# Full-row products on TensorE as two column tiles of 128x64 instead of one of 128x128

## The chip, the cores and the metric

The kernel runs on one core of one Trainium2 chip. The metric is the device time of one execution in microseconds (us). The kernel before takes 568.61 us (median of three runs: 567.25, 568.61 and 568.85).

## What is computed

The program is a cross-attention block in float32. There are 8 batches of 256 query tokens, 256 context tokens and 1024 features in 32 heads of 32. The context serves as keys and as values.

```
x = (hidden - mu) * rsqrt(var + 1e-5) * ln_gamma + ln_beta
Q = split_heads(x @ Wq.T);  K = V = split_heads(ctx)
probs = softmax(where(mask, Q K^T * 32**-0.5, -inf))
out = hidden + (probs @ V) @ Wout.T
```

Everything in it that is a matrix product runs on TensorE: the query product `x @ Wq.T`, the scores `Q K^T`, the values `probs @ V`, and the output product with `Wout`.

## The kernel before

The work is cut into 64 slots, `n` from 0 to 63: 8 batches times 8 groups of 4 heads. The loop `for n in range(N)` writes every engine's work by hand, so that in slot `n` TensorE does, in this order:

- `scores(n + 1)`: 16 products into four PSUM banks, each of 32 rows of the array (one head) by 64 columns (half of a block of 128 queries), with 256 columns of keys streaming through. Its matmuls are on line 487.
- `values(n - 2)`: 32 products of 64 rows by 32 columns, with 128 columns streaming. Line 638.
- products that use all 128 rows and 128 columns of the array, one after another: query products (`first_q`, `make_q` and `query_product`, lines 290, 345 and 447), and output products (`product_steps`, line 722, and `end_steps`, line 789).

From batch 2 on the query product, and from the first batch on the output product, is computed by Strassen's scheme (Winograd's form): 7 half-size products in place of 8, with sums of the operands made by GpSimd (`sum_x`, `sum_at`, `sum_wq`, `sum_wo`). `query_product` makes one of the seven: 16 matmuls of a 128x128 block of weights, with 128 columns of x streaming through each. `product_steps` is called with a list of steps from the table `STEPS`, which spreads 28 matmuls over nine slots. One matmul there has a 128x128 block of attention as its stationary operand and streams 512 columns of Wout.

In float32 each matmul that is written stands in the trace as two MATMUL records and two LDWEIGHTS records (loads of the stationary operand), 8290 of each in all. The stationary operand and the streamed one come from SBUF, the sum lands in PSUM.

The other engines work on the softmax of slot n + 1 (VectorE and ScalarE read the scores out of PSUM, GpSimd divides), copy products out of PSUM, and add the residual. The SyncE queue issues nearly all transfers. Instructions on one engine run in the written order. TensorE's first matmul of a product waits for its operands and for its PSUM bank. The bank tiles that matter: `pq` (one bank, query products, and the first output product of a batch), `po` (one bank, output products), `sc` (four banks, scores), `pv` (two banks, values).

Of the kernel before, what the change touches and what calls it, by code (L numbers as in the profile page):

```python
# [51 lines left out]
P = 128  # L52
# [7 lines left out]
def xattn_kernel(  # L60
# [10 lines left out]
    nc = tc.nc  # L71
# [138 lines left out]
        load_wo(which, pair)  # L210


    xnTs, mvs, rstds = {}, {}, {}

    sts = {}
# [68 lines left out]
    def first_q(s, chunks=range(NC)):  # L284

        if s == 0:
            pqs[0] = ps_q.tile([P, 512], F32, tag="pq", name="pq_0")
        cols = ds(0, P) if s == 0 else ds(P, P + 1)
        for c in chunks:
            nc.tensor.matmul(  # L290
                pqs[0][:, cols], wq[:, 0, c, :], xnT0[:, c, cols],
                start=(c == chunks[0]), stop=(c == chunks[-1]),
            )
        nc.scalar.activation(qa[:, 0, cols], pqs[0][:, cols], AF.Copy, scale=NEG_SCALE)
# [41 lines left out]
    def make_q(n, second=False, chunks=range(NC)):  # L336
        b, o = divmod(n, NQ)
        if chunks[0] == 0:
            if second:
                bank = ps_o.tile([P, 512], F32, tag="po", name=f"pq_{n}")  # L340
            else:
                bank = ps_q.tile([P, 512], F32, tag="pq", name=f"pq_{n}")
            pqs[n] = bank[:, : S + 1] if b == 0 else bank[:, :S]
        for c in chunks:
            nc.tensor.matmul(  # L345
                pqs[n], wq[:, o, c, :], xnTs[b](c), start=(c == 0), stop=(c == NC - 1),
            )

# [34 lines left out]
    def weights(name, o):  # L383

        if name == "ring":
            return ring[:, o]
        first, k = W_AT[name]
        return wq[:, first + o, ds(k, NK)]
# [30 lines left out]
    def x_part(b, name):  # L419

        if name in ("S1", "S3"):
            return sums_x[:, 0]
        if name == "S2":
            return sums_x[:, 1]
        s, k = {"A11": (0, 0), "A12": (0, 1), "A21": (1, 0), "A22": (1, 1), "S4": (1, 0),
                "P1": (0, 0)}[name]
        return to_move[b][:, :, ts(k, NK), s, :].rearrange("p a c k -> p c a k")
# [9 lines left out]
    def query_product(b, p):  # L437
        name, which, begins = Q_PRODUCTS[p]
        if b == SPLIT and name == "A11":
            which = "B11"  # L440
        if begins:
            pqs[b] = ps_q.tile([P, NK, P], F32, tag="pq", name=f"pq_{b}_{name}")
        x_ = x_part(b, name)
        for o in range(NK):
            w = weights(which, o)
            for c in range(NK):
                nc.tensor.matmul(  # L447
                    pqs[b][:, o, :], w[:, c], x_[:, c], start=begins and o + c == 0,
                    stop=c == NK - 1, skip_group_check=True,
                )  # L450
# [232 lines left out]
    def operand(b, name):  # L683

        if name in ("S2", "S1"):
            return s2s[b]
        s, k = {"A11": (0, 0), "A12": (0, 1), "A21": (1, 0), "A22": (1, 1),
                "S3": (1, 0), "S4": (0, 1)}[name]
        return ats[b, k][:, :, s].rearrange("p c a k -> p c (a k)")
# [14 lines left out]
    def product_steps(b, steps):  # L704
        for step in steps:
            p, c = divmod(step, NK)
            name, which, begins = PRODUCTS[p]
            begins = begins or b in P1_ASIDE and name == "A12"
            po = pos.get(b)
            if b == B - 2 and name in ("A12", "S2"):  # L710

                begins = name == "A12"
                if begins and c == 0:
                    po_q[0] = ps_q.tile([P, 512], F32, tag="pq", name=f"po_{b}_{name}")
                po = po_q[0] if begins else po
            elif b in P1_ASIDE and name == "A11":
                if c == 0:
                    p1_pos[b] = ps_q.tile([P, 512], F32, tag="pq", name=f"po_{b}_{name}")
                po = p1_pos[b]
            elif begins and c == 0:  # L720
                po = pos[b] = ps_o.tile([P, 512], F32, tag="po", name=f"po_{b}_{name}")
            nc.tensor.matmul(  # L722
                po, operand(b, name)[:, c], wo[:, which, c],
                start=begins and c == 0, stop=c == NK - 1,
                skip_group_check=not begins,
            )
# [46 lines left out]
    def end_operand(name):  # L773
        return end_sums[name] if name in end_sums else operand(B - 1, name)
# [11 lines left out]
    def end_steps(po, name, which, chunks, begins=(), cols=slice(0, 512)):  # L786

        for c in chunks:
            nc.tensor.matmul(  # L789
                po, end_operand(name)[:, c], wo[:, which, c, cols],  # L790
                start=c in begins, stop=True, skip_group_check=True,
            )
# [100 lines left out]
    nc.gpsimd.tensor_copy(xnT0[:, :, S], bet)  # L893
    ln_norm(0, 1, nc.vector)
    first_q(0, early + late)
    mask_bias(0)
    transpose_x0(1)
# [6 lines left out]
    ])  # L904
    next(first)
    first_q(1)
    make_q(1, second=True, chunks=range(2))
    next(first)
    scores(0, (1,))
    make_q(1, second=True, chunks=range(2, NC))  # L910
    make_q(2)
    for _ in first:
        pass
# [21 lines left out]
    def project_steps(n, place):  # L935
        for one in steps.get((n, place), ()):
            product_steps(*one)


    for n in range(N):  # L940
# [47 lines left out]
        if n in products:  # L988
            query_product(*products[n])
            copies.append(partial(copy_product, *products[n]))  # L990
# [67 lines left out]
        if N - NQ + 2 < n < N - 1:  # L1058

            c = n - (N - NQ + 3)  # L1060
            if c == 0:
                last = ps_q.tile([P, 512], F32, tag="pq", name="po_last")
            end_steps(last, "A11", B11, (c,), (0,))
# [20 lines left out]
    for c in range(2):  # L1084
        end_steps(to_c11, "A12", B21, (c,), (0,))
        end_steps(to_c21, "A22", T4, (c,), (0,))
# [78 lines left out]
```

## Time and profile before

The profiled execution took 567.12 us; its span from the first to the last instruction is 565.3 us.

| engine | busy us | share of the span | instructions |
|---|---|---|---|
| TensorE matmuls (PE) | 560.3 | 99% | 8290 |
| TensorE weight loads (PEld) | 385.3 | 68% | 8290 |
| VectorE (DVE) | 467.0 | 83% | 1716 |
| ScalarE (ACT) | 423.8 | 75% | 1464 |
| GpSimd (POOL) | 395.7 | 70% | 636 |

The granted TensorE clock is full (0.999). The 16 DMA engines moved 211 GB/s on average. Matmuls are pipelined: a record lasts longer than the distance to the next one, so the pace of a stream is read from starts, or from how long a run of equal matmuls takes, and not from the mean length of one.

### The profile page before, as it was taken

How to read it: one execution, taken by the hardware profiler on the slowest of the kernel's cores; microseconds unless marked ns; L12 is line 12 of the kernel's file. 1: busy time of each engine (PE TensorE's matmuls, PEld its weight loads, DVE VectorE, ACT ScalarE, POOL GpSimd, SP SyncE). 2: the span in 40 equal slices, each digit the busy share in tenths (PEclk: the TensorE clock that was granted, in tenths of full speed). 3: DMA queues.
4: the chain of work that ended last, by engine and by line, in shares of the span. 5: the costliest groups of instructions: out<-in, count | busy, mean ns of one | idle time of the engine just before them, and what ended most of it. 6: DMA issues, size and time to landing. Idle time of an engine off the chain costs nothing.

```text
span 565.3 us, 22379 instructions
## 1 busy us (share of the span) xinstructions
PE 560.3 (99%) x8290; PEld 385.3 (68%) x8290; DVE 467.0 (83%) x1716; ACT 423.8 (75%) x1464; POOL 395.7 (70%) x636
## 2 busy tenths in 40 slices
PE   8999999999999999999999999999999999999997
PEld 8777775767766767667766776667766767754454
DVE  5889889999897988978888888988888877879923
ACT  3699989997767866787777867778776876769920
POOL 2688887899777666867568665777648657448780
PEclk9999999999999999999999999999999999999999
DMA  8967667966698677877779667887658874536651
GB/s 310 397 178 203 173 188 216 296 179 177 199 311 255 206 196 228 253 206 207 206 225 283 191 174 221 242 264 197 172 155 257 244 202 134 149 105 183 205 169 74
DMA packets 47228, 119.17 MB, mean 211 GB/s; under 512 B 8976, under 2 KB 9744, under 8 KB 47120
## 3 DMA queue, kind: packets, MB, share of 16 engines
q1 hardware_dynamic: 46976, 117.74, 69.9%
q8 instruction: 66, 1.08, 0.9%
q14 instruction: 42, 0.34, 0.2%
q10 hardware_dynamic: 144, 0.01, 0.0%
HBM read 66.33 MB, written 11.53 MB: 138 GB/s over the span
## 4 chain that ended last, share of the span: by engine, by line
PE 82%; POOL 5%; DVE 5%; ACT 3%; issue 2%; DMA 2%; SPq 0%; DVEq 0%; POOLq 0%; ACTq 0%
PE po_S L722 21%; PE pq_A L447 19%; PE pv L638 11%; PE sc L487 10%; PE po_A L722 10%; PE pq_S L447 8%; PE po_end L789 3%; ACT e L530 2%; POOL e L545 2%; DVE e L526 2%; DVE pT L551 2%; PE po_last L789 1%; DMA pT<-pT 1%; POOL wo L182 1%; POOL wq L366 1%
## 5 line engine op out<-in xcount | busy, mean ns | idle before, releaser
L545 POOL TENSOR_SCALAR e<-e,rden 128x256 f32<-128x256 f32 x466 | 216.6, 483 | 123.2 <-DVE rden L537 120.6
L530 ACT ACTIVATE e<-e,mn 128x256 f32<-128x256 f32 x512 | 254.1, 502 | 45.2 <-DVE mn L526 44.8
L551 DVE STREAM_TRANSPOSE pT<-e 128x512 f32<-128x512 f32 x256 | 178.9, 704 | 36.6 <-POOL e L545 32.3
L526 DVE CUSTOM_DVE_ANT_0 e<-sc,mb 128x256 f32<-128x256 f32 x512 | 185.2, 415 | 24.8 <-PE sc L487 24.5
L557 ACT COPY pc<-pT 128x512 f32<-128x512 f32 x128 | 79.0, 617 | 55.3 <-DVE pT L551 35.7
L530 ACT ACTIVATION_READ_ACCUMULATOR e<-e,mn 128x1 f32 x512 | 98.5, 192 | 0.0
L638 PEld LDWEIGHTS pv<-pT,v 64*32 64x32 f32 x4096 | 57.1, 105 | 25.7 <-ACT pc L557 11.5
L722 PE MATMUL po_S<-wo,at 128*128 128x512 f32 x152 | 74.3, 606 | 0.0
L638 PE MATMUL pv<-pT,v 64*32 64x128 f32 x4096 | 74.2, 274 | 0.0
L487 PE MATMUL sc<-k,qa 32*64 32x256 f32 x2048 | 71.9, 387 | 0.1
L487 PEld LDWEIGHTS sc<-k,qa 32*64 32x64 f32 x2048 | 37.7, 131 | 45.5 <-issue 32.1
L722 PE MATMUL po_A<-wo,at 128*128 128x512 f32 x128 | 59.4, 605 | 0.0
L345 PE MATMUL pq<-xnT,wq 128*128 128x256 f32 (+1 forms) x240 | 55.0, 384 | 0.1
L447 PEld LDWEIGHTS pq_A<-xnT,wq 128*128 128x128 f32 x416 | 48.5, 192 | 6.2 <-issue 5.0
L345 PEld LDWEIGHTS pq<-xnT,wq 128*128 128x128 f32 x240 | 44.6, 190 | 8.5 <-issue 1.2
L722 PE MATMUL po_S<-wo,s 128*128 128x512 f32 x104 | 50.2, 607 | 0.0
L447 PE MATMUL pq_A<-xnT,wq 128*128 128x128 f32 x416 | 48.5, 275 | 0.0
L537 DVE RECIPROCAL rden<-den 128x2 f32<-128x2 f32 x256 | 38.1, 149 | 6.6 <-ACT e L530 5.6
L526 DVE DVE_READ_ACCUMULATOR2_ANT mn<- 128x1 f32 x512 | 42.4, 83 | 0.0
L722 PEld LDWEIGHTS po_A<-wo,at 128*128 128x128 f32 x128 | 22.9, 189 | 25.7 <-issue 24.7
L722 PEld LDWEIGHTS po_S<-wo,at 128*128 128x128 f32 x152 | 25.5, 190 | 19.6 <-issue 19.6
L755 POOL TENSOR_TENSOR r<-r,p 128x512 f32<-128x512 f32 x24 | 30.7, 1281 | 4.8 <-DMA r<-in_x_dram 3.9
(102 smaller groups left out, 666.7 us busy)
## 6 DMA issues: line engine op xcount, KB each, us to landing
v<-in_kv_dram SPq DMA_DIRECT2D x32, 512.0 KB, 4.6
pT<-pT SPq DMA_DIRECT2D x128, 128.0 KB, 3.2
pT<-pc SPq DMA_DIRECT2D x128, 128.0 KB, 4.3
ring<-kept_T SPq DMA_DIRECT2D x20, 512.0 KB, 5.5
k<-in_kv_dram SPq DMA_DIRECT2D x32, 256.0 KB, 4.2
x<-in_x_dram SPq DMA_DIRECT2D x15, 512.0 KB, 5.6
r<-in_x_dram SPq DMA_DIRECT2D x28, 256.0 KB, 5.0
out_dram<-r SPq DMA_DIRECT2D x28, 256.0 KB, 3.5
```

The source lines that it names most:

```text
L345: nc.tensor.matmul(pqs[n], wq[:, o, c, :], xnTs[b](c), start=(c == 0), stop=(c == NC - 1),)
L447: nc.tensor.matmul(pqs[b][:, o, :], w[:, c], x_[:, c], start=begins and o + c == 0, stop=c == NK - 1, skip_group_check=True,)
L487: nc.tensor.matmul(scs[n][j][ts(w, P // 2), s, :], qa[r, n % NQ, ds(s * P + w * P // 2, P // 2)], ks[n - n % 2][r, n % 2, :], start=True, ...
L526: nc.vector.tensor_tensor_reduce(out=e[:, s, :], in0=pss[j][:, s, :], in1=mbs[n // NQ], scale=1.0, scalar=NO_SCORE, op0=ALU.add, op1=ALU.m ...
L530: nc.scalar.activation(e[:, s, :], e[:, s, :], AF.Exp, bias=mn[:, s : s + 1], scale=-1.0, accum_out=den[:, s : s + 1],)
L537: nc.vector.reciprocal(rden, dens[j])
L545: engine.tensor_scalar(es[j][:, s, :], es[j][:, s, :], rden[:, s : s + 1], 1.0, ALU.mult, ALU.mult,)
L551: nc.vector.transpose(pT[:, :, :, j, :, :].rearrange("p a i s k -> p (a i) s k"), es[j].rearrange("p s (b t) -> p b s t", t=K),)
L557: nc.scalar.copy(pc[:, :, ts(j, 2)], pT[:, 1, :, ts(j, 2)])
L638: nc.tensor.matmul(pvs[n][r][j * HD : (j + 1) * HD], vs[n - n % 2][ts(r, 2 * K), i, ds(n % 2 * P + j * HD, HD)], pT[ts(r, 2 * K), :, i, j, ...
L722: nc.tensor.matmul(po, operand(b, name)[:, c], wo[:, which, c], start=begins and c == 0, stop=c == NK - 1, skip_group_check=not begins,)
L755: nc.gpsimd.tensor_tensor(r, r, p1s[b], ALU.add)
```

## The change

A helper `product(out, stationary, moving)` takes the place of `nc.tensor.matmul` at the five places that use the whole array. It writes two matmuls. The first has columns 0 to 63 of the stationary block and writes PSUM partitions 0 to 63; the second has columns 64 to 127 and writes partitions 64 to 127. Both stream the same moving operand, and both carry the same start and stop flags.

```diff
+    def product(out, stationary, moving, **flags):
+
+        for w in range(2):
+            nc.tensor.matmul(
+                out[ts(w, P // 2)], stationary[:, ts(w, P // 2)], moving, **flags
+            )
+
@@ first_q
-            nc.tensor.matmul(
+            product(
                 pqs[0][:, cols], wq[:, 0, c, :], xnT0[:, c, cols],
@@ make_q
-            nc.tensor.matmul(
+            product(
                 pqs[n], wq[:, o, c, :], xnTs[b](c), start=(c == 0), stop=(c == NC - 1),
@@ query_product
-                nc.tensor.matmul(
+                product(
                     pqs[b][:, o, :], w[:, c], x_[:, c], start=begins and o + c == 0,
@@ product_steps
-            nc.tensor.matmul(
+            product(
                 po, operand(b, name)[:, c], wo[:, which, c],
@@ end_steps
-            nc.tensor.matmul(
+            product(
                 po, end_operand(name)[:, c], wo[:, which, c, cols],
```

Scores, values and transposes keep their matmuls. No other engine's instructions change. On TensorE, the place behind a slot's values shows what stands there. Before, with `pq_S` the query product of Strassen's sum S1, `po_S` the output product of S2, and `sc` the next scores:

```order
L722 MATMUL po_A_3995<-wo,at_1_3577 128x512
L447 MATMUL pq_S_4130<-sx,ring 128x128 x16
L722 MATMUL po_S_4222<-wo,s_2_4065 128x512 x2
L487 MATMUL sc_0_4226<-k_3927,qa 64x256 x2
L487 MATMUL sc_1_4227<-k_3927,qa 64x256 x2
```

The same place in the list after the change (line 216 is the helper's matmul, line 494 that of the scores):

```order
L216 MATMUL po_A_4415<-wo,at_1_3953 64x512 x2
L216 MATMUL pq_S_4554<-sx,ring 64x128 x32
L216 MATMUL po_S_4662<-wo,s_2_4488 64x512 x4
L494 MATMUL sc_0_4668<-k_4343,qa 64x256 x2
L494 MATMUL sc_1_4669<-k_4343,qa 64x256 x2
```

The query product has 32 matmuls of 64 columns in place of 16 of 128, the output product four in place of two, and nothing stands in another order.

## The prediction

> **What bounds the kernel now.** I read the page's totals first, then the waits of TensorE, then its busy time in one batch, then the chain in one slot.
>
> ```profile
> span 565.3 us, 22379 instructions
> PE 560.3 (99%) x8290; PEld 385.3 (68%) x8290; DVE 467.0 (83%) x1716; ACT 423.8 (75%) x1464; POOL 395.7 (70%) x636
> PE busy L119 <- POOL ring masks.py:199: 1.4, 1, 1.4
> PE px L273 <- DVE ring L886: 0.4, 1, 0.4
> 303.90:371.60 67.70, 67.70 (x1050) 46.97 (x1049) 58.29 (x213) 51.43 (x180) 46.86 (x81) 1.00 0.77 220
> ```
>
> The third and fourth rows are all the waits of TensorE matmuls for another engine: at the warm-up and the first transposes, lines 119 and 273. The fifth is one batch, 303.9 to 371.6 us: columns are the window's length, then busy time of PE, PEld, DVE, ACT and POOL, then clock 1.00 and the transfers' share. PE is busy for all of it, the next engine (DVE) for 58.29 of 67.70 us. So PE's own pace is the time, and a busy share of 99% says nothing of what that pace could be: matmuls overlap. That is read from the chain of a slot, from 181 to 195 us:
>
> ```profile
> 181.29 1.72 PE po_S L722 x4
> 183.01 1.05 PE sc L487 x32
> 184.06 1.08 PE pv L638 x64
> 185.15 1.91 PE po_S L722 x4
> 187.06 3.57 PE pq_A L447 x32
> ```
>
> The reader sees PE following PE without a hole. Output products cost 1.72/4 = 0.430 us a record (512 columns), query products 3.57/32 = 0.1116 us (128 columns). The `po_S x4` behind the values costs 0.19 us more than the other one. Two things in this stream have to do with the width of the stationary operand.
>
> **First: the weight load that nothing hides.** When the array goes from values back to the full-row form, the first matmul has no earlier matmul to load its weights behind. Its record is longer than the others of its kind (minimum, median and maximum, in ns):
>
> ```profile
> L722 PE MATMUL po_S<-wo,s x104: 592/592/697, 103.8 to 529.0; 128*128 128x512 f32 x104
> L447 PE MATMUL pq_S<-sx,ring x192: 273/275/377, 100.1 to 442.7; 128*128 128x128 f32 x192
> L487 PE MATMUL sc<-k,qa x2048: 374/374/427, 12.2 to 531.1; 32*64 32x256 f32 x187
> L638 PE MATMUL pv<-pT,v x4096: 268/269/295, 36.8 to 549.1; 64*32 64x128 f32 x196
> ```
>
> The excess is 697 - 592 = 105 or 377 - 275 = 102 ns with a stationary operand of 128 columns, 427 - 374 = 53 with 64 (scores), and 295 - 269 = 26 with 32 (values). It goes by the columns of one load, although eight loads of scores start at once. With 64 columns the full-row products should pay 53 as well, so each return saves 104 - 53 = about 51 ns.
>
> How many returns are there? Each slot has one, behind its values:
>
> ```profile
> 0.00:100.10 100.10, 10.40 (x576) 7.99 (x576) 1.00 0.75 238
> 100.10:565.30 465.20, 63.83 (x3520) 49.09 (x3520) 1.00 0.70 205
> ```
>
> These are the values' records before and after 100.1 us. At 64 records a slot they are 9 and 55 returns. After 100.1 us: 55 x 51 ns = 2.8 us. Bounds: 0, if the two loads of a pair use one path one after the other (53 + 53), and 55 x 105 = 5.8 us if the load vanished.
>
> **Second: the pace of the query products.** A stream of 128 columns has been seen to go faster than 111.6 ns:
>
> ```profile
> 11.19 1.04 PE L271 MATMUL px<-ring,x 128*128 128x128 f32 x8
> L271 PEld LDWEIGHTS px<-ring,x x8: 139/141/142, 11.1 to 11.8; 128*128 128x128 f32 x8
> L271 PE MATMUL px<-ring,x x8: 272/272/273, 11.2 to 12.0; 128*128 128x128 f32 x8
> L447 PEld LDWEIGHTS pq_S<-sx,ring x192: 186/192/192, 100.1 to 442.6; 128*128 128x128 f32 x192
> 0.00:565.30 565.30, 157.56 (x1344) 156.10 (x1344) 1.00 0.71 211
> ```
>
> Eight transposes take 1.04 us, the last of which is 0.272: (1040 - 272)/7 = 109.7 ns apart. Their loads last 141 ns; those of the query products 192, and here a matmul record is 275 long in place of 272. So each query matmul is held by 2 to 3 ns by the load ahead of it. Loads of 64 columns are shorter:
>
> ```profile
> L487 PEld LDWEIGHTS sc<-k,qa x2048: 127/132/133, 12.2 to 530.9; 32*64 32x64 f32 x187
> ```
>
> At 132 ns, below the transposes' 141, they should hold nothing. The last row counts the records of line 447: 1344. Side by side in two tiles, the streams of twice as many records are as long as these 1344. I take 2.4 ns each, the middle of 111.6 - 109.7 = 1.9 and 275 - 272 = 3: 3.2 us (bounds 0, if the pair's loads share a path, and 1344 x 3 = 4.0). The output products' 430 ns are too long for a load to hold them, so there I count nothing.
>
> **What is added, and whether the tiles run side by side.** The full-row lines have 1344 + 392 + 240 + 66 + 32 records, 2074 in all:
>
> ```profile
> 0.00:565.30 565.30, 187.27 (x392) 67.67 (x392) 1.00 0.71 211
> 0.00:565.30 565.30, 54.98 (x240) 44.57 (x240) 1.00 0.71 211
> 0.00:565.30 565.30, 26.38 (x66) 11.82 (x66) 1.00 0.71 211
> 0.00:565.30 565.30, 4.00 (x32) 3.73 (x32) 1.00 0.71 211
> 105.60 1.12 PE L487 MATMUL sc<-k,qa 32*64 32x256 f32 x32
> 105.60 0.47 PE L487 MATMUL sc<-k,qa 32*64 32x256 f32 x8
> 106.65 1.16 PE L638 MATMUL pv<-pT,v 64*32 64x128 f32 x64
> ```
>
> (Lines 722, 345, 789 and 290, then scores and values in one slot.) The change adds 2074 more. They cost nothing only if two column tiles over the same rows run at once. Scores are just that, twice over: four row groups by two column tiles. Its 32 records of 256 columns take 1.12 us. One batch of eight starts within 0.47 - 0.427 = 0.04 us, so 6 ns apart, and four such batches make the 32 records: (1.12 - 0.47)/3 = 0.217 us a batch, which is the time of one stream of 256 columns (430/2 = 215), not of two. So column tiles do run at full pace. Their start 6 ns apart is the price: at each end of a full-row stretch the second tile is done 6 ns later, 55 x 6 = 0.3 us.
>
> The sequencer keeps up: in values it feeds 64 pairs of load and matmul in 1.16 us, 18 ns each; a pair of column tiles needs one per 55 ns. Even the 2074 new pairs, exposed at 18 ns, would be 37 us; what hides them is 55 ns of streaming behind every one. Instruction fetch grows by a quarter at most:
>
> ```profile
> q8 instruction: 66, 1.08, 0.9%
> ```
>
> That is 0.3 MB more beside 119 MB. The change of form at scores and values stays, as often as before.
>
> **Who could be late next.** After 100.1 us the sum is -2.8 - 3.2 + 0.3 = -5.7 us, 0.1 us a slot. Before that, one wait is already near the end of its cover:
>
> ```profile
> 98.92 1.13 PE L722 MATMUL po_A<-wo,at 128*128 128x512 f32 x2
> 100.11 1.08 PEld L447 LDWEIGHTS pq_S<-sx,ring 128*128 128x128 f32 x9 [0.89 <-POOL sx L435]
> 171.69 0.30 PEld L722 LDWEIGHTS po_S<-wo,s 128*128 128x128 f32 x2 [0.21 <-DVE r L764]
> 10.00:100.00 90.00, 89.82 (x1269) 68.01 (x1267) 79.97 (x308) 78.60 (x264) 71.41 (x97) 1.00 0.75 235
> ```
>
> At 100.11 us the query product waits for GpSimd's sum `sx`: from 98.92 us, two records with an unhidden load need 0.105 + 2 x 0.430 = 0.97, and 1.19 passed. So what the 9 returns before it save (9 x 45 = 0.4 us) is waited for there, and I count it as nothing. Later waits of this kind (the load at 171.69 us, whose bank VectorE has to read first) are tenths of a microsecond in a batch. VectorE has 9.4 us to spare in a batch, against 0.8 us that the batch becomes shorter.
>
> Span: 565.3 - 5.7 = 559.6 us. The profiled execution took 567.12, 1.8 over its span, and is 1.5 us below the median of the runs, 568.61. So the median comes out at 568.61 - 5.7 = 562.9 us.
>
> **The rivals.**
>
> *The tiles wait for each other in the written order (slower).* Each written matmul is two records on one tile. If records start strictly in order, the first tile's second record must start before the other tile's first. In a steady stream the tiles still overlap, shifted by one record, but each record starts 6 ns behind its neighbour (1037 pairs x 2 x 6 ns = 12 us), and each full-row stretch ends one record later, mostly with 512 columns (some 50 x 0.43 = 22 us). That is 562.9 + 34 = 597 us. It decides as soon as one held record holds the next tile's. Against it stand the scores: 16 written matmuls of two records would then take at least 16 x 0.215 = 3.4 us and take 1.12. Chance 5%.
>
> The Trainium skill's page "TensorE: Matmul & The Clock Gate", in the section "Part 3: Packing small matmuls — row/col tiling", says that matmuls start and end in strict program order and that only weight loads are pulled ahead. By that rule alone this rival would hold and the sum would be +28 us. The trace does not agree where tiles differ: 1.12 us for the scores' 32 records.
>
> *Column tiles over 128 rows don't overlap at all.* Then 2074 records are exposed: at least 1344 x 0.11 + 392 x 0.43 = 317 us on top. The scores cover all 128 rows with two column tiles, which speaks against it. 2%.
>
> *The sequencer or the fetch of instructions falls behind* by a few ns at each of 1037 added matmuls: at 10 ns, +10 us, 573. For it: nothing but the doubled count. 4%.
>
> *The pair's loads share one path.* Then 53 + 53 is the old 105 and two loads of 64 columns hold as one of 128 did; 568.9 us, no change. The scores' eight loads in parallel speak against it, but they belong to 32 rows each, where these have 128. 8%.
>
> *Another engine takes up half the gain*, through more waits like those at 100.11 and 171.69: 565.8 us. 8%. *The load is hidden wholly and the hold is 3 ns:* 568.61 - 5.8 - 4.0 + 0.3 = 559.1 us. 5%.
>
> **How the numbers follow.** My forecast, 562.9 us, has 68%; its own range is 561 to 565, from the spread of the three runs (1.6 us) and the terms' bounds. With the two partial cases, 559.1 and 565.8, that is 81% for faster by over 0.3% (below 566.9), which is about what this kernel's measurement can tell from no change. Within 0.3%: 8%, the shared path. Slower: 5 + 2 + 4 = 11%. The range from 558.5 to 568.5 us holds the forecast, both partial cases and most of the shared path.
>
> **What would show it.** Right: full-row records at 64 columns; line 447's run of a slot (now 64 records) in 3.50 us in place of 3.57; the first matmul behind the values 53 ns over its kind's median, not 105; scores and values unchanged; a batch in 66.9 us in place of 67.7. Wrong: a run of 64 query records in over 3.57 us, or 0.43 us of half-used array ahead of the scores, as strict order would have it; waits of PE for `sx`, `po` or `pT` that were not there.

## The result and the profile after

The change was timed in two comparisons, each with runs of the kernel before beside it. Ratios, here and below, are of runs in the chip's faster state; in this document that leaves out a single run, the longest of the four tiles (602.99 us).

| comparison | with the change, us | before, us | ratio, 95% interval |
|---|---|---|---|
| first | 565.4 (564.03 to 566.44, 5 runs) | 567.91 (5 runs) | 0.995 [0.993, 0.997] |
| repeated | 567.28 (565.64 to 569.43, 12 runs) | 567.32 (17 runs) | 0.9993 [0.9972, 1.0014] |

So it is worth between nothing and 2.5 us, where 5.7 had been forecast. The two intervals do not overlap, and no run tells why the comparisons differ. What TensorE does per matmul went as forecast, but the time was lost again in waits that the kernel before did not have. The page of the kernel after (total, engines, the queue that fetches instructions):

```profile
span 563.6 us, 26534 instructions
PE 556.2 (99%) x10364; PEld 350.8 (62%) x10364; DVE 467.4 (83%) x1716; ACT 423.4 (75%) x1464; POOL 394.8 (70%) x636
q8 instruction: 82, 1.34, 1.0%
```

PE has 2074 records more, and is busy 4.1 us less. Instructions came in 82 pieces of 16 KB in place of 66. Next, one batch of the kernel after, in the view of busy times by window (columns as in the prediction), and the shortest, median and longest records of three groups:

```profile
303.25:370.03 66.78, 66.78 (x1330) 43.68 (x1328) 58.04 (x213) 51.30 (x180) 45.95 (x81) 1.00 0.77 223
L216 PE MATMUL po_S<-wo,s x208: 592/592/644, 104.9 to 527.5; 128*64 128x512 f32 x104
L216 PE MATMUL pq_A<-sx,ring x384: 272/273/324, 134.8 to 475.6; 128*64 128x128 f32 x192
L216 PEld LDWEIGHTS pq_S<-sx,ring x384: 132/137/138, 101.0 to 442.1; 128*64 128x64 f32 x192
```

This batch has no wait in it: 66.78 us where the same batch took 67.70 before. The load that nothing hides is 644 - 592 = 52 ns (105 before), the query records are 273 ns (275), the loads 137 (192). Now the chain of the next slots, from 370 us on:

```profile
370.20 3.50 PE pq_S L216 x64
373.69 1.72 PE po_S L216 x8
375.41 1.05 PE sc L494 x32
376.46 1.09 PE pv L645 x64
377.55 1.87 PE po_S L216 x8
379.41 2.61 PE pq_S L216 x47
382.03 1.69 issue
383.71 1.20 PE pq_S L216 x17
```

The query product takes 3.50 us (3.57 before), the output product behind the values 1.87 (1.91). Then a query product breaks off after 47 of its 64 records. For 1.69 us TensorE has nothing to wait for that the profile knows, and nothing to do ("issue"). All waits of TensorE matmuls in this execution:

```profile
PE pq_S L216 <- issue: 1.7, 1, 1.7
PE busy L119 <- POOL ring masks.py:199: 1.3, 1, 1.3
PE po_S L216 <- DVE r L771: 0.7, 1, 0.7
PE pv L645 <- DMA pT<-pc: 0.4, 1, 0.4
PE sc L494 <- ACT qa L301: 0.2, 1, 0.2
```

Before, only the two waits ahead of the first scores were there. The third and fourth rows, a wait for the bank `po` and one for `pT`, are signs that the prediction had named for being wrong. The first row is the supply of instructions. In the 9.5 us ahead of the break, 371.5 to 381.0 us, the transfers' view has only two queues that moved anything, and q8 is not one of them:

```profile
q1 hardware_dynamic: 1094, 2.61, 89.6%
q14 instruction: 1, 0.01, 0.2%
```

The next piece of q8 begins between 381.10 and 381.15 us. The view of this window of 0.05 us counts the whole transfer, as a share of what 16 engines have in it:

```profile
q8 instruction: 1, 0.02, 159.0%
```

So the piece took 1.59 x 16 x 0.05 = 1.27 us and landed at 382.4 us, 0.4 us after TensorE had run dry (379.41 + 2.61 = 382.02), and TensorE went on 1.3 us after the landing. The piece before it had begun at 369.8 us, 11.3 us earlier. In the kernel before, two pieces at the same place begin at 371.0 and 381.2 us, nearly as far apart, and TensorE did not stop. One thing that differs is how much it uses up meanwhile. The same 9.5 us in both kernels, first after and then before (columns as above, then the share of the DMA engines and GB/s):

```profile
371.50:381.00 9.50, 9.50 (x188) 6.32 (x184) 8.11 (x31) 8.84 (x31) 6.44 (x14) 1.00 0.90 275
371.50:381.00 9.50, 9.50 (x138) 6.58 (x137) 7.77 (x34) 8.85 (x31) 6.36 (x13) 1.00 0.87 258
```

That is 94 written matmuls in place of 69, where a piece holds some 63 (5182 written matmuls in 82 pieces). Over the whole span a piece lasts 565.3/66 = 8.6 us before, and 563.6/82 = 6.9 us after the change. This is no bound by itself: in the version "Only where it pays", 222 records (111 written matmuls) pass between the starts of two pieces, 254.28 and 264.48 us, without a stop. How much TensorE has in store when a piece comes late, the profile does not show.

### The profile page after: what moved, and what is told of

Read it like the earlier page. It is cut to its first block, busy times and chain, and to the rows that moved or that the text cites. A ratio compares the mean times of both kernels' runs of the same rounds, so it can differ in the third digit from the quotient of the medians.

```text
span 563.6 us, 26534 instructions
## 1 busy us (share of the span) xinstructions
PE 556.2 (99%) x10364; PEld 350.8 (62%) x10364; DVE 467.4 (83%) x1716; ACT 423.4 (75%) x1464; POOL 394.8 (70%) x636
## 4 chain that ended last, share of the span: by engine, by line
PE 77%; DVE 6%; POOL 6%; DMA 5%; SPq 2%; issue 2%; ACT 2%; DVEq 0%; POOLq 0%
PE po_S L216 17%; PE pq_A L216 16%; PE pv L645 10%; PE sc L494 9%; PE po_A L216 8%; PE pq L216 6%; PE pq_S L216 6%; PE po_end L216 3%; DVE pT L558 2%; DMA pT<-pT 2%; DMA r<-in_x_dram 2%; ACT e L537 1%; POOL e L552 1%; DVE e L533 1%; PE po_last L216 1%
## 5 line engine op out<-in xcount | busy, mean ns | idle before, releaser
L216 PE MATMUL po_S<-wo,at 128*64 128x512 f32 x304 | 73.9, 599 | 0.0
L216 PE MATMUL po_A<-wo,at 128*64 128x512 f32 x256 | 58.6, 599 | 0.0
L216 PE MATMUL pq<-xnT,wq 128*64 128x256 f32 (+3 forms) x544 | 58.4, 369 | 0.0
L216 PEld LDWEIGHTS pq_A<-xnT,wq 128*64 128x64 f32 x832 | 46.6, 137 | 7.1 <-issue 5.7
L216 PE MATMUL po_S<-wo,s 128*64 128x512 f32 x208 | 49.8, 600 | 0.7 <-DVE r L771 0.7
L216 PEld LDWEIGHTS pq<-xnT,wq 128*64 128x64 f32 x544 | 36.8, 136 | 19.1 <-issue 1.7
L216 PE MATMUL pq_A<-xnT,wq 128*64 128x128 f32 x832 | 47.8, 273 | 0.0
L216 PEld LDWEIGHTS po_A<-wo,at 128*64 128x64 f32 x256 | 16.9, 136 | 30.0 <-issue 28.7
L216 PEld LDWEIGHTS po_S<-wo,at 128*64 128x64 f32 x304 | 20.3, 136 | 21.9 <-issue 21.6
```

Of the source, the lines that this page charges most:

```text
L216: nc.tensor.matmul(out[ts(w, P // 2)], stationary[:, ts(w, P // 2)], moving, **flags)
```

## The experiments

Two theories for the waits, in the names of the texts on record. **Supply:** the added matmuls need more instructions, and these come late where transfers are dense. **Period:** a shorter batch lets transfers and residual adds come too late, whatever the number of instructions. Rivals: the waits belong to one bad execution; the fetch has a pace of its own, whatever the traffic.

### The changed kernel once more

No edit.

> The changed kernel once more, for a second profile. In the first one TensorE's own pace gained 5.4 us (full-row stretches without their waits), and some 3 us of new waits of TensorE took half of it: 1.7 us with nothing to wait for but its next instruction (at 381.8 us), 0.7 us for the residual add that frees the output bank (at 171.8 us), 0.4 us for a transposing transfer (at 90 us). Theory 'supply' (each added matmul has to be fetched as 256 bytes of instructions, and the fetch comes late where the transfers are dense): again 1 us or more of TensorE without an instruction, at a place where the DMA engines are full, perhaps another one; time 564 to 566. Theory 'period' (a shorter batch brings transfers and residual adds too late, whatever the number of instructions): the same two waits for the residual and the transfer at the same places, no gap in the supply. Rival 'one bad execution': waits under 1 us in all and a time of 562 to 563.

Measured: 567.28 us, ratio 0.9993 [0.9972, 1.0014]. TensorE's longest waits, but for the warm-up's:

```profile
PE po_S L216 <- DVE r L771: 2.5, 2, 1.3
PE pq_S L216 <- issue: 1.4, 1, 1.4
PE pq_S L216 <- DMA ring<-kept_T: 0.7, 1, 0.7
```

The gap of supply is there again, in the same product (at 383.9 us), and the wait for VectorE's store has grown to 2.5 us in two batches. So waits of this kind belong to the changed kernel, and their size differs between the two profiles. The spread of the times says nothing about that: 3.8 us in the twelve runs of the change, 5.0 in the seventeen of the kernel before. Both theories have a part, and 567.28 us lies above what either had expected. The timeline at 171 us shows what the store waits for:

```profile
171.43 1.26 POOL L762 TENSOR_TENSOR r<-r,p 128x512 f32<-128x512 f32 x1 [4.21 <-ACT e L537]
172.73 0.69 DVE L771 TENSOR_TENSOR r<-po_A,r 128x512 f32<-128x512 f32 x1 [3.33 <-POOL r L762]
173.48 1.08 PE L216 MATMUL po_S<-wo,s 128*64 128x512 f32 x4 [1.34 <-DVE r L771]
```

The residual is added on GpSimd, then the store on VectorE frees the one output bank, then TensorE begins the next output product. GpSimd had stood idle for 4.21 us before the add. The row names ScalarE's `e` as what ended this; the load of the residual had been issued at 166.45 us (164.52 in the kernel before), and the experiment with an earlier load, below, shows that it is this load that counts. In the first profile of the changed kernel the row names it:

```profile
170.70 1.28 POOL L762 TENSOR_TENSOR r<-r,p 128x512 f32<-128x512 f32 x1 [2.62 <-DMA r<-in_x_dram]
```

### Less work without more instructions

```diff
             for c in range(NK):
+                if p % 2 == 0 and o == NK - 1 and c == NK - 2:
+                    continue
                 nc.tensor.matmul(
```

> The kernel before, with one of the 16 matmuls left out in four of the seven query products of each batch from 2 on (so those products are incomplete). That takes 24 x 223 ns = 5.4 us from TensorE's work, as much as the change took, without adding an instruction. Theory 'supply': the time falls by the whole 5 to 5.4 us, ratio 0.990 to 0.991. Theory 'period': TensorE meets the same late transfers and residual adds, and the time falls by 2 to 3 us as it did with the change, ratio 0.995 to 0.996.

Measured: 563.05 us (6 runs) against 567.32, ratio 0.9924 [0.9906, 0.9942]: 4.3 of the 5.4 us arrive. No gap of supply; of the period's waits one is there:

```profile
PE busy L119 <- POOL ring masks.py:199: 1.3, 1, 1.3
PE po_S L724 <- DVE r L766: 1.3, 1, 1.3
PE px L273 <- DVE ring L888: 1.1, 1, 1.1
```

So a TensorE that is faster by as much, with the old number of instructions (65 pieces of q8), keeps four fifths. It lies between the two expectations, nearer to *supply*. The period has its own share: the same store, at 306 us.

### Four column tiles

```diff
-        for w in range(2):
+        for w in range(4):
             nc.tensor.matmul(
-                out[ts(w, P // 2)], stationary[:, ts(w, P // 2)], moving, **flags
+                out[ts(w, P // 4)], stationary[:, ts(w, P // 4)], moving, **flags
```

> The full-row products as four column tiles of 128x32. TensorE's own pace: the load that nothing hides falls from 53 to 26 ns at 55 returns (-1.5 us), the ends of stretches come 12 ns later (+0.7 us), so -0.8 us against two tiles. Instructions: 1037 x 2 more matmuls than with two tiles, so some 1.86 MB to fetch in place of 1.34. Theory 'supply': the gaps in supply become more and longer, and the time is above that of two tiles, 567 us or more. Theory 'period': 564 to 565 us, as with two tiles. If a tile of 32 columns loses pace at 512 or 128 columns, the runs of query products show it (over 3.50 us each).

Measured: 598.81 us (592.37 to 602.99), ratio 1.0514 [1.0469, 1.056]. The page's span and instruction queue, TensorE's waits, and three pieces of the chain around 203 us:

```profile
span 596.8 us, 34830 instructions
q8 instruction: 114, 1.87, 1.4%
```

```profile
PE pv L645 <- issue: 12.0, 12, 3.5
PE pq_S L216 <- issue: 5.0, 8, 1.3
PE pq_A L216 <- issue: 1.9, 5, 0.6
PE po_S L216 <- issue: 1.4, 1, 1.4
```

```profile
201.46 0.99 PE po_S L216 x8
202.46 3.49 PE pq_A L216 x128
205.95 1.72 PE po_S L216 x16
```

Where instructions are at hand, four tiles are as fast as the forecast for their pace says: 3.49 us a query product, and 0.99 us for an output matmul behind the values (1.01 with two tiles). Most of the rest is lack of instructions: 12.0 + 5.0 + 1.9 + 1.4 = 20.3 us in these rows, and 1.3 us in two smaller ones. That is 28 stops. The trace has the start and length of every piece of q8: each of the 28 ends 1.2 to 1.7 us after a piece has landed, as do the stop of 1.69 us above and the one in its second profile, while the pieces themselves begin 3 to 9 us apart there. So these stops are waits for q8. The largest one, in the timeline, is inside the values, which the edit does not touch:

```profile
306.50 1.09 PE L645 MATMUL pv<-pT,v 64*32 64x128 f32 x56
311.08 0.42 PE L645 MATMUL pv<-pT,v 64*32 64x128 f32 x8 [3.49 <-issue]
```

TensorE stops 56 records into 64 and has nothing for 3.49 us. The piece that it waits for begins at 308.6 us and takes 1.2. Behind this stop the granted clock (the column ahead of the last two) falls to half for 3.4 us, and the output products go at half their pace:

```profile
312.00:315.00 3.00, 3.00 (x20) 0.87 (x16) 1.79 (x5) 2.93 (x12) 1.69 (x4) 0.50 0.96 331
```

That is another 1.7 us. The stops of 1.4 and 1.7 us with two tiles have no such fall behind them. One of the five runs of the change in the first comparison and two of the twelve in the second have a mean granted clock of 0.997, as a fall of this length would make it (3.4 x 0.5 us of 565), and none of the seventeen of the kernel before has; whether a long stop stood in them is not known. *Supply* holds; *period* alone, at 564 to 565 us, falls.

### The same kernels with fewer transfers

```diff
                 for half, slot in enumerate(slots):
-                    rings[slot].append(partial(load_ring, name, half))
+                    pass
```

This leaves out the 30 loads of weight tables, in the kernel before, in the changed one, and in the one with four tiles.

> The kernel before without the loads that bring kept weight tables back into the tile 'ring' (30 transfers of 512 KB, of 118 MB in all; the query products of the later batches then multiply by stale weights). It is the reference for the next run. TensorE's work is unchanged and it waits for next to nothing, so 566 to 567.5 us on every theory.

> The changed kernel without the same loads (stale weights as there). Theory 'late where transfers are dense' (TensorE's instructions and the residuals arrive late because the DMA engines are full, as they are from 364 to 381 us): with 15.7 MB fewer transfers the gaps of supply and the waits for the residual shrink to under 1 us, and the kernel is 4.5 to 5.5 us below the run without loads before it, ratio to the kernel before 0.990 to 0.992. Rival 'too many instructions whatever the traffic': TensorE is still without an instruction for 1.4 us or more and the gain stays under 3 us.

> Four column tiles of 128x32, without the 30 table loads (stale weights as before). With all transfers four tiles take 598.8 us, of which the profile shows over 21 us as TensorE without an instruction. Theory 'the fetch is late because the DMA engines are full': fewer transfers give most of it back, 560 to 580 us (TensorE's own pace would be 560.5). Rival 'the fetch has a pace of its own that four tiles exceed': still over 590 us.

Measured: 566.98 us for before (ratio to the full one 0.9988 [0.9974, 1.0003]), 561.77 us for the change (0.9899 [0.9872, 0.9927]), 581.62 us for four tiles (1.026 [1.021, 1.0309]). With two tiles, as the first theory expected, the supply gap is gone and so is the wait for the store. The waits and the first query product of three batches in the chain:

```profile
PE busy L119 <- POOL ring masks.py:199: 1.3, 1, 1.3
PE pq_S L216 <- POOL sx L442: 0.7, 1, 0.7
PE sc L494 <- ACT qa L301: 0.2, 1, 0.2
```

```profile
235.18 3.50 PE pq_S L216 x64
301.97 3.49 PE pq_S L216 x64
368.75 3.49 PE pq_S L216 x64
```

A batch takes 66.79 and 66.78 us, and the change is worth 566.98 - 561.77 = 5.2 us: nearly the forecast 5.7. The one wait for `sx` that is left is the one at 100 us that the prediction had named. For four tiles 581.62 us lies between the two expectations (560 to 580, over 590): 17 of 31 us come back, and 11.8 us of "issue" are left in its profile, of 21.6. So the traffic has a large part in the lack of instructions. That the fetch has a pace of its own for the rest is possible and not shown, since the DMA engines were still about 60% busy. The edit takes away two things at once, traffic and a place in the SyncE queue where these loads wait for TensorE. Instructions come over a queue of their own (q8), so the shorter stops of the four tiles go with the traffic. For the residual the two are not separated. With two tiles the missing gap is one profile's word, and a profile with all loads, that of "Only where it pays", has none either.

### An earlier residual

```diff
-            if i < 4:
+            if 0 < i < 4:
                 between.append(partial(load_res, b, *((0, 0), (0, 1), (1, 1), (1, 0))[i]))
+        if i == NQ - 1 and b + 1 < B - 1:
+            between.append(partial(load_res, b + 1, 0, 0))
```

> The changed kernel with each batch's first residual tile loaded one slot earlier (slot 7 of the batch before in place of slot 0). The wait of the output product for VectorE's store at 171.8 and 240.2 us (2.5 us in the second profile) goes back through GpSimd's add to this load. Theory 'period': this wait goes, the gap of supply stays (1.4 to 1.9 us): 564 to 565.5 us. If the wait comes from GpSimd being late with its other work, it stays, and the time is that of the change, 565 to 567.5.

> The same earlier residual load in the kernel before. There TensorE waits for that store by 0.2 us in one batch only, so no change is expected: 567 to 568 us. If it falls by over 1.5 us, the earlier load is worth something for itself, and the gain of the previous run is not that of the change.

Measured: with the change 565.88 us (562.94 to 570.66, 12 runs), ratio 0.9976 [0.9946, 1.0006]; in the kernel before 567.36, 0.9999 [0.9984, 1.0015], no change, as expected. The wait for the store is gone, and GpSimd's add stands without idle time before it, so it was the residual's load that the store had waited for:

```profile
167.25 1.28 POOL L762 TENSOR_TENSOR r<-r,p 128x512 f32<-128x512 f32 x1
```

Other waits stand in its place (changed kernel with the earlier load):

```profile
PE pv L645 <- DMA k<-in_kv_dram: 1.2, 1, 1.2
PE pq_S L216 <- DMA ring<-kept_T: 0.8, 2, 0.6
PE pq_A L216 <- issue: 0.4, 1, 0.4
PE pv L645 <- issue: 0.3, 1, 0.3
```

All of them are transfers or instructions that came late, at other places. The time is 0.4 us above the 564 to 565.5 expected if the wait went, the gap of supply is smaller than expected, and the interval takes in no change.

### Only where it pays

The changed kernel with the earlier residual, and `nc.tensor.matmul` again in `first_q` and `make_q`.

> The changed kernel with the earlier residual load, and with the first two batches' query products (lines 290 and 345 of the kernel before) left at 128x128. Before 100 us a faster TensorE only waits for GpSimd's sum, so what is given up there (13 returns x 45 ns = 0.6 us) should cost nothing, and 136 of the 1037 added matmuls go. Theory 'supply': 564 to 565.5 us, at or a little below the earlier residual load alone. If the first 100 us had been worth their 0.6 us, 566 to 567.

Measured: 565.86 us (561.85 to 569.37, 12 runs) against 567.56, ratio 0.9973 [0.995, 0.9997]. The time lies between the two expectations (564 to 565.5, 566 to 567). It is as good as the previous one with 136 matmuls fewer, so column tiles in the first 100 us bought nothing that can be seen. Among the versions with all loads and 12 runs it has the best interval, 0.3% below the kernel before, and it is not told apart from the change itself.

### Output products alone

Column tiles at lines 722 and 789 of the kernel before only.

> Only the output products (lines 722 and 789 of the kernel before) as two column tiles; the query products stay 128x128. Now the form changes inside a full-row stretch, at 73 places. If a change of form between two full-row forms costs what one to or from the scores costs (92 ns of drain and then a load that nothing hides, 53 or 105 ns: 0.17 us), that is +12.4 us, against 51 returns x 52 ns = -2.6 us: 577 to 579 us. If such a change is free: 565 to 566 us, less than the whole change gains, because the query products keep their 111.6 ns.

Measured: 577.96 us (4 runs), ratio 1.0182 [1.0162, 1.0202], as the first case of its expectation said. In the chain a query product now takes 3.77 us where it took 3.57, and an output product behind one 1.87 where it took 1.72:

```profile
189.31 3.77 PE pq_A L454 x32
201.00 1.87 PE po_S L216 x8
```

That is 0.20 us for the change to 128x128 and 0.15 for the one to 128x64. TensorE waits for no instruction here, so this is the price of changing the form, and not of supply.

## Why the prediction was right or wrong

- **What bounds the kernel: right.** A run of TensorE without waits is the time, and where the waits stayed away a batch took 66.78 us, with 66.9 forecast.
- **The load that nothing hides: right.** 52 ns after, 53 forecast.
- **The hold of the query products: right.** A product takes 3.49 to 3.50 us, 3.50 forecast.
- **Side by side: right.** The rival of strict order (597 us) and the one without overlap would need a half-used array ahead of the scores or products of double length; the chain has neither. The rival of a shared load path falls with the 52 ns.
- **"The sequencer keeps up" and "Instruction fetch grows by a quarter at most": this step failed.** The added instructions were weighed by their bytes (0.3 MB beside 119 MB), and by the sequencer's pace with instructions at hand (18 ns), and the sum put them at nothing. What the runs show in their place: TensorE uses up a 16 KB piece sooner (6.9 us in place of 8.6) while the next came no sooner where the DMA engines were full (11.3 us in place of 10.2). In the two profiles of the change that cost 1.7 and 1.4 us, in the same product. The rival that named it had 4% and was priced at 10 ns a matmul throughout; the runs show it as rare stops of 1.4 to 1.7 us, and with four tiles as 28 stops.
- **"Who could be late next": the place was right, the size was not, and this is the second term that the sum put at nothing.** The store that frees the output bank was named, with tenths of a microsecond in a batch. It measured 0.7 and 2.5 us in an execution; with the other late transfers, 0.4 and 0.7 us, that is 1.1 us in the first profile, and 3.2 in the second, more than the lack of instructions there. VectorE's 9.4 us of spare time in a batch was beside the point, because what is late is the residual's transfer, not VectorE. A TensorE faster by 5.4 us without any added instruction lost 1.1 of it.
- **The first 100 us counted as nothing: right**, as far as the experiment that leaves those products at 128x128 can show it.
- **The sum:** -5.7 us of pace is -5.2 with fewer transfers. In the full kernel it is -2.5 in one comparison and nothing in the other. The forecast's own range, 561 to 565, held neither time. The wide range, 558.5 to 568.5, held both times, but by its width: its upper part was there for a shared load path, which the 52 ns rule out, and not for waits of this size. The rival in which another engine takes half the gain came close in its time, 565.8 us, and its mechanism is part of what happened. The sum also starts from 568.61 us, the median of three runs, and the kernel before came out at 567.2 to 567.9 later.

What stays open: why the piece of instructions came so late at that place (full DMA engines are shown, the order in which they serve the queues is not), how much TensorE had in store then, what the other stops and slower stretches of the four tiles add up to beyond the 21.6 us of these rows, and how much of the difference between the two comparisons is the chance of where these waits fall.

## What to carry to other kernels

In this kernel, narrower column tiles shortened the weight load behind a change of form and freed short products from their loads, and TensorE took the gain; but every matmul that is added has to be fetched. Before splitting, count the instruction pieces on the page and what the split adds to them; after it, look for "issue" among TensorE's waits, and whether such a wait ends just behind a late piece. The average time of a piece does not tell where TensorE stops: 66 and 82 pieces cost next to nothing and up to 1.7 us here, 114 pieces more than 20. With TensorE busy 99% of the time and DMA engines full in places, a gain in pace was kept only in part, because transfers and buffers did not arrive sooner as well. And all full-row products of one stretch need the same form: with two forms in it the kernel lost 10.6 us.

## What the runs showed of the hardware

- Two and four column tiles over the same 128 rows run at full pace: 3.49 to 3.50 us a query product either way, and 1.72 us for an output product of 8 records of 512 columns, which is four times 0.43.
- An unhidden weight load goes by the columns of one tile: 105, 52 and 26 ns for 128 (full rows before), 64 (after) and 32 (values), though the values' loads start several at once.
- A change of form between two full-row forms costs 0.15 to 0.20 us (output products alone).
- TensorE can run out of instructions in the middle of a product, for 3.49 us at most here, and the profile shows this only as "issue". The word alone does not prove it: an "issue" of 0.5 us in the kernel before with the earlier residual ends 5.8 us after the last piece of q8 landed.
- After stops of 2.5 us (four tiles with fewer transfers) and 3.49 us (four tiles) the granted clock was 0.50 for 3.4 us; after stops of up to 1.69 us it stayed at 1.00.
